# Layer 3 of a graph network kernel: odd key blocks' exponentials added to the even block by an accumulating DMA, sums taken once per pair of blocks, layer 0's residual added by DMA, and a new order of the work

## The chip, the cores and the metric

The kernel runs on one core of a Trainium2 chip. The metric is device time in microseconds (us). The kernel before takes 2258.46 us, the median of three runs (2258.31 to 2259.9). A core has five engines that run side by side, each through its own queue of instructions in order: PE (TensorE, matrix products; its weight loads are listed as PEld), DVE (VectorE), ACT (ScalarE), POOL (GpSimd) and SP (SyncE). Here SP and POOL issue the DMA transfers, which 16 DMA engines carry out.

## The reference

Sixteen graphs of 1024 nodes with 128 features pass through four layers. Each layer ends with `x = layernorm(x + layer(x, adj))`; the adjacency is 0 or 1, about 3% of it ones.

```python
def layer0(X, A, W, a):                       # one head of 128
    H = X @ W
    e = leaky_relu((H @ a[:U])[:, None] + (H @ a[U:])[None, :], 0.2)
    return relu(softmax(e + where(A > 0, 0, -1e9)) @ H)
# layer 1: the same with 8 heads of 16 and elu at the end
# layer 2: mean over the neighbours of x @ W_r, plus x @ self_w.T + self_b, then layernorm, gamma, beta, relu
def layer3(X, A, W):                          # 4 heads of 32
    Wh = einsum('bsf,hfd->bhsd', X, W)
    scores = einsum('bhsd,bhtd->bhst', Wh, Wh) / sqrt(32)
    attn = softmax(where(A > 0, scores, -9e15))
    return einsum('bhst,bhtd->bhsd', attn, Wh)    # heads joined to 128 features
```

## The kernel before

The 1024 nodes are 8 blocks of 128 (`NB = 8`), in two halves of 512. All four layers of a graph work on the same eight mask tiles `m` (one per key block, 8-bit, loaded and converted from `adj` by transfers that POOL issues, L557).

*Layer 0* (`layer0`). DVE makes the weights `z` of each key block (L636), PE multiplies them with `hd` (L648) into two PSUM accumulators `acc1`, ACT divides and applies relu (`share`, L669) into `x1`. DVE then adds the graph's input rows, which SP has loaded into the tile `x0` (L624), by one tensor_tensor per half (L689). The layernorm (`layernorm`: squares L430, `about`, a Newton step, application L468) starts from sums that `share` and the first products give, so it needs no pass of its own for the mean.

*Layer 1* (`layer1`). For each of two groups of 4 heads and each key block DVE makes four `z` of 1024 (L788), and PE multiplies them, four products of 32 columns side by side (L796). Results are copied to `oT1` by ACT (L826), transposed by PE, divided by DVE. *Layer 2* (`layer2`) is products with the masks (L928).

*Layer 3* (`before3`, `layer3`). Queries are taken in two halves of 512. For each key block j: ACT turns the mask into a gap (L1066); PE makes the scores of 4 heads into the two PSUM tiles of the pool `wk` (L1076 for the gap, L1087 for the products); ACT takes their exponentials into two SBUF tiles of the pool `z3`, two heads each (L1123); PE multiplies these tiles (`weighted`, L1102). Keys lie on the partitions, so both the weighted values and the softmax's denominators are products: for each head one with `hh` (32 columns of values) and one with `ones` (32 columns of ones). A tile `acc3` holds two heads, values and denominators in alternate stripes of 32 partitions. After 8 blocks ACT copies both accumulators to `oT3` (L1139), PE transposes them, DVE divides (`share`, L1150 and L1153) and adds the layer's input (L1164).

*Order.* No loop order is written out. Every piece of work is a `step` with an engine, an estimated duration, a due time, the buffers it reads and writes, and a lag after which its results count as there. `Plan.run` simulates the engines with these estimates and emits the instructions in the order in which its simulated engines would start them: of those steps that could start about now, the one with the earliest due time. A pool's places are given out in that simulation too, so which buffer a step uses, and whom it waits for on the chip, comes from it. `SAME` and `URGENT` shift due times (for PE steps of the same kind as the one before, and for ACT and DVE steps that hold PSUM), `LATER1` and `LATER3` those of the products that follow the weights. Consecutive graphs are due `PERIOD` apart, so layer 3 of one graph runs beside layers 0 and 1 of the next. On the chip the emitted order is fixed for each engine; semaphores do the waiting.

The functions with the line numbers of the profile:

Of the kernel before, what the change touches and what calls it, by code (L numbers as in the profile page):

```python
# [24 lines left out]
ALU = mybir.AluOpType  # L25
# [3 lines left out]
P = 128  # L29
HALF = 512  # L30
# [46 lines left out]
class Plan:  # L77
# [8 lines left out]
    SAME = 0.0  # L86
    URGENT = 61.2
    AHEAD = 4322.0
# [136 lines left out]
def tile_binary(  # L225
# [3 lines left out]
    xT_in: bass.AP,  # L229
    adjT: bass.AP,  # L230
# [61 lines left out]
    LATER1 = -3.8  # L292
    LATER3 = 48.7
# [35 lines left out]
    places("z3", 4, [P, 2, HALF])  # L329
    places("oT1", 1, [P, N])  # L330
    places("oT3", 1, [P, N])
    places("x0", 1, [P, NB, P])
# [218 lines left out]
    def before0(b, due):  # L551
        G = graphs[b]
        G["m"] = [Buf("m", f"m_{b}_{j}") for j in range(NB)]
        for j, m in enumerate(G["m"]):
            step(
                "POOL", 0.55, due - 60 + 5 * j,
                lambda m=m, j=j: nc.gpsimd.dma_start(out=m.t, in_=adjT[b, j * P : (j + 1) * P, :]),  # L557
                [], [m], lag=5.0, floor=12.0 + 3 * j if b == 1 else max(due - 60 + 5 * j, 0.0),
            )
        x0 = G["x"] = Buf("x0", f"x0_{b}")  # L560
# [63 lines left out]
        step("SP", 2.0, due, lambda: nc.sync.dma_start(out=x0.t, in_=natural(x[b])), [], [x0], lag=2.5)  # L624

    def layer0(b, due):
# [4 lines left out]
        for half in range(2):  # L631
# [32 lines left out]
            for n in range(2):  # L664
# [23 lines left out]
                "DVE", 0.6, at,  # L688
                lambda ks=ks: nc.vector.tensor_tensor(y.t[:, ks, :], y.t[:, ks, :], G["x"].t[:, ks, :], ALU.add),  # L689
                [G["x"]], [(y, half)],  # L690
# [87 lines left out]
    def layer1(b, due, span):  # L778
# [3 lines left out]
        for g in range(2):  # L782
# [39 lines left out]
            oT, pt, rd = Buf("oT1", "oT1"), Buf("wk", "pb1"), little("rd1", [P, NB, G1, 1])  # L822
# [31 lines left out]
    def last1(b, due):  # L854

        G = graphs[b]
        o, x1, e = G["x2"], G["x1"], Buf("oT1", "e")
# [131 lines left out]
    def before3(b, due):  # L989
# [41 lines left out]
        sq, norms, bound = Buf("oT3", "sq"), little("norms", [P, NB * H3]), little("bound", [P, 1])  # L1031
# [23 lines left out]
    def layer3(b, due, span):  # L1055
# [3 lines left out]
        for half in range(2):  # L1059
            cols = slice(half * HALF, (half + 1) * HALF)  # L1060
            av = [Buf("acc3", f"av3_{g}") for g in range(2)]
# [34 lines left out]
            def weighted(j, g, z, av=av):  # L1096

                for h in range(2):
                    at = D3 * (2 * g + h)
                    for n, lhsT in enumerate((hhs[j // HB].t[:, j % HB, at : at + D3], ones)):  # L1100
                        at = 64 * h + 32 * n
                        nc.tensor.matmul(  # L1102
                            av[g].t[at : at + 32, :],
                            lhsT=lhsT,
                            rhs=z.t[:, h, :],
                            start=j == 0,
                            stop=j == NB - 1,
                        )

            for j in range(NB):  # L1110
# [4 lines left out]
                step("ACT", 0.68, at - 8, lambda j=j, gap=gap, f=missing: f(j, gap), [m[j]], [gap])  # L1115
# [4 lines left out]
                for g in (0, 1):  # L1120
                    step(
                        "ACT", 1.0, at,
                        lambda g=g, sc=sc, zs=zs: nc.scalar.activation(  # L1123
                            zs[g].t.rearrange("p h n -> p (h n)"), sc[g].t, AF.Exp, bias=low.t, scale=S3
                        ),
                        [sc[g], low], [zs[g]],
                    )
                for g in (0, 1):
                    step(
                        "PE", 0.87, at + LATER3, lambda j=j, g=g, z=zs[g], f=weighted: f(j, g, z),  # L1130
                        [zs[g], hhs[j // HB]], [av[g]], mode="32 columns",
                    )
            at = due + span * (half + 1) / 2
            oT, pt, rd = Buf("oT3", "oT3"), Buf("wk", "pb3"), little("rd3", [P, 2 * HB, 2, 1])
            o = Buf("rest", "o3")
            for g in range(2):
                step(
                    "ACT", 0.48, at,
                    lambda g=g, oT=oT, av=av: nc.scalar.copy(oT.t[:, g * HALF : (g + 1) * HALF], av[g].t),  # L1139
                    [av[g]], [(oT, g)],  # L1140
                )
# [6 lines left out]
            def share(pt=pt, rd=rd, o=o):  # L1148
                pn = blocks(pt.t).rearrange("p m (c w) -> p m c w", c=2)
                nc.vector.reciprocal(rd.t, pn[:, :, :, D3 : D3 + 1])  # L1150
                for g in range(2):
                    of_g = slice(g * HB, (g + 1) * HB)
                    nc.vector.tensor_tensor(  # L1153
                        o.t.rearrange("p k (h d) -> p k h d", h=H3)[:, :, 2 * g : 2 * g + 2, :],
                        pn[:, of_g, :, :D3],
                        rd.t[:, of_g].to_broadcast([P, HB, 2, D3]),
                        ALU.mult,
                    )

            step("DVE", 1.07, at, share, [pt], [rd, o])  # L1160
# [22 lines left out]
    PERIOD = 129.0  # L1183
    weights(-198)
    for b in range(B):
        at = b * PERIOD
        at0 = 25 if b == 1 else at
        before0(b, at0 - 50)
        layer0(b, at0)
        before1(b, at + 25)  # L1190
        layer1(b, at + 99, 111)
        last1(b, at + 165)
        layer2(b, at + 165)
        before3(b, at + 223)
        layer3(b, at + 321, 108)
# [579 lines left out]
def tile_adj_resnorm(ctx: ExitStack, tc: tile.TileContext, x, adjT, *weights_and_out, xT):  # L1775
# [3 lines left out]
    tile_binary(tc, x, xT, adjT, *weights_and_out, wrong)  # L1779
# [44 lines left out]
```

## Time and profile before

| | |
|---|---|
| median of three runs | 2258.46 us |
| profiled execution | span 2254.1 us |
| busy, PE / DVE / ACT / POOL | 2074.9 / 1902.1 / 1743.5 / 130.9 us |
| PE products of layer 3 after the exponentials (L1102), with `hh` / with `ones` | 2048 / 2048 rows |
| residual of layer 0 on DVE (L689) | 32 instructions, 683 ns each |
| mask loads (L557) | 128, 540 ns to issue |
| DMA, mean over the span | 53 GB/s |

The profile is one execution. Its span (first to last recorded instruction) is 4.4 us below the median of the runs, which are timed from outside. An engine's busy time is the time in which at least one of its instructions ran. A PE product of 32-bit data appears as two rows. Groups of instructions are listed by line, engine and operation, as output<-inputs, with their count, their busy time, the mean duration of one, then the idle time of the engine just before them and who ended it. In the slices, the span is cut into 40 parts and each digit is a busy share in tenths. The chain is followed back from the last instruction to what released each one.

### The profile page before, as it was taken

The numbers are of one execution on the slowest core, as the hardware profiler recorded it, in microseconds if no ns is written. First come the engines' busy times: TensorE is split into PE (matmuls) and PEld (weight loads), VectorE is DVE, ScalarE is ACT, GpSimd is POOL, SyncE is SP. The second block draws the span as 40 slices with busy tenths as digits, with TensorE's granted clock in tenths as the row PEclk, the third lists the DMA queues.
The fourth block names the chain that finished last, engine by engine and source line by source line (L and its number), as shares of the span: only waits on it lengthen the run. The fifth ranks groups of instructions, "written<-read, shape, count | busy, mean of one in ns | idle before, by whom it ended". The sixth has DMA issues, their size and how long they took to land.

```text
span 2254.1 us, 55458 instructions
## 1 busy us (share of the span) xinstructions
PE 2074.9 (92%) x23472; PEld 971.1 (43%) x23472; DVE 1902.1 (84%) x2854; ACT 1743.5 (77%) x4376; POOL 130.9 (6%) x187
## 2 busy tenths in 40 slices
PE   4857999999999999999999999999999999998876
PEld 4613545353534544363544535353454436242311
DVE  2899999989989989999999998998999999997211
ACT  3413769878787879878787987878787987868786
POOL 1010000100000000000000010000000000000000
PEclk9878999999999999999999999999999999999999
DMA  6122130312323040222314031232304122200000
GB/s 97 59 77 36 37 85 18 92 38 77 48 86 48 20 100 25 86 39 86 48 32 99 18 91 38 77 48 85 50 20 96 29 77 39 77 11 11 2 11 12
DMA packets 80851, 119.86 MB, mean 53 GB/s; under 512 B 7384, under 2 KB 58704, under 8 KB 80592
## 3 DMA queue, kind: packets, MB, share of 16 engines
q1 hardware_dynamic: 62160, 99.43, 13.1%
q0 software_dynamic: 18432, 16.79, 9.0%
q8 instruction: 186, 3.05, 0.6%
q14 instruction: 73, 0.60, 0.1%
HBM read 157.55 MB, written 8.97 MB: 74 GB/s over the span
## 4 chain that ended last, share of the span: by engine, by line
PE 52%; DVE 24%; ACT 20%; issue 3%; DMA 1%; POOL 0%; DVEq 0%; POOLq 0%; ACTq 0%
DVE z L788 18%; PE acc L648 10%; PE acc L1102 9%; PE acc L796 9%; PE wk L928 8%; ACT z L1123 6%; PE wk L1087 6%; PE wk L366 4%; ACT junk L430 4%; ACT x L468 3%; PE wk L375 3%; ACT gap L1066 3%; PE wk L1076 2%; PE wk L1001 1%; ACT hd L620 1%
## 5 line engine op out<-in xcount | busy, mean ns | idle before, releaser
L788 DVE SCALAR_TENSOR_TENSOR z<-R,q,m 128x1024 f32<-128x1024 f32 x1024 | 1248.9, 1279 | 16.1 <-PE acc L796 8.3
L1123 ACT ACTIVATE z<-wk,low 128x1024 f32<-128x1024 f32 x512 | 545.3, 1105 | 58.2 <-PE wk L1087 56.7
L796 PE MATMUL acc<-z,hh 128*32 128x512 f32 x4096 | 512.3, 612 | 46.1 <-DVE z L788 44.6
L1102 PE MATMUL acc<-z,hh 128*32 128x512 f32 x2048 | 516.2, 604 | 33.4 <-ACT z L1123 33.4
L1102 PE MATMUL acc<-z,ones 128*32 128x512 f32 x2048 | 516.1, 604 | 0.0
L430 ACT ACTIVATE junk<-x,off 128x128 f32<-128x128 f32 x640 | 256.2, 400 | 230.8 <-DVE off L424 214.6
L1087 PE MATMUL wk<-whT,turn 32*64 32x512 f32 x4096 | 286.3, 615 | 0.0
L468 ACT ACTIVATE x<-x,shift,rstd 128x128 f32<-128x128 f32 x640 | 259.3, 485 | 7.7 <-DVE shift L462 7.6
L648 PEld LDWEIGHTS acc<-hd,z 128*128 128x128 f32 x2048 | 237.3, 193 | 34.8 <-ACT x L669 12.6
L796 PEld LDWEIGHTS acc<-z,hh 128*32 128x32 f32 x4096 | 110.6, 110 | 326.8 <-issue 194.6
L648 PE MATMUL acc<-hd,z 128*128 128x129 f32 x2048 | 244.7, 278 | 5.9 <-DVE z L636 4.5
L1102 PEld LDWEIGHTS acc<-z,hh 128*32 128x32 f32 x2048 | 97.9, 109 | 279.1 <-issue 190.2
L928 PE MATMUL wk<-y,m 128*128 128x128 bf16 (+1 forms) x3072 | 182.9, 220 | 24.5 <-ACT z L1123 19.9
L1066 ACT ACTIVATE gap<-m,neg_one 128x512 bf16<-128x512 fp8e5 x256 | 183.4, 718 | 20.6 <-DMA m<-in_adj_dram 20.6
L928 PEld LDWEIGHTS <-m 128*128 128x128 fp8e5 x3072 | 181.0, 98 | 37.0 <-issue 27.3
L636 DVE SCALAR_TENSOR_TENSOR z<-R,q,m 128x512 f32<-128x512 f32 x240 | 162.8, 746 | 1.0 <-DMA R<-rows 1.0
L1102 PEld LDWEIGHTS acc<-z,ones 128*32 128x32 f32 x2048 | 97.6, 109 | 83.0 <-issue 83.0
L1076 PEld LDWEIGHTS <-far 32*32 32x32 bf16 x4096 | 35.7, 88 | 210.0 <-issue 198.2
L430 ACT ACTIVATION_READ_ACCUMULATOR junk<-x,off 128x1 f32 x640 | 120.4, 188 | 0.0
L1076 PE MATMUL wk<-gap,far 32*32 32x512 bf16 x4096 | 113.3, 386 | 3.4 <-DVE rest L1153 1.7
L557 POOL DMA_DIRECT2D m<-in_adj_dram x128 | 68.3, 540 | 796.2 <-ACT gap L1066 765.8
L1087 PEld LDWEIGHTS wk<-whT,turn 32*64 32x64 f32 x4096 | 59.8, 130 | 58.6 <-issue 58.6
(119 smaller groups left out, 1859.7 us busy)
## 6 DMA issues: line engine op xcount, KB each, us to landing
R<-rows SPq DMA_DIRECT2D x139, 512.0 KB
m<-in_adj_dram POOLq DMA_DIRECT2D x128, 128.0 KB, 5.6
xT<-in_xT_dram SPq DMA_DIRECT2D x32, 256.0 KB
x<-in_x_dram SPq DMA_DIRECT2D x16, 512.0 KB
out_dram<-x SPq DMA_DIRECT2D x15, 512.0 KB
rows<-rT SPq DMA_DIRECT2D x16, 32.0 KB
out_dram<-x SPq DMA_DIRECT2D x2, 256.0 KB
z<-in_L_gnn_a_dram SPq DMA_DIRECT2D x2, 128.0 KB
```

Source lines behind the costliest of these rows:

```text
L430: nc.scalar.activation(junk.t, y.t[:, k, :], AF.Square, bias=off.t[:, k : k + 1], accum_out=squared.t[:, k : k + 1])
L468: nc.scalar.activation(y.t[:, k, :], y.t[:, k, :], AF.Identity, bias=shift.t[:, k : k + 1], scale=rstd.t[:, k : k + 1])
L636: nc.vector.scalar_tensor_tensor(z.t[:, (j % 2) * HALF : (j % 2 + 1) * HALF], in0=R0.t[:, cols], scalar=q.t[:, j : j + 1], in1=m[j].t[:, c ...
L648: nc.tensor.matmul(av[k // 2].t.rearrange("p (k c) -> p k c", k=2)[:, k % 2, : P + 1], lhsT=z.t[:, at : at + P], rhs=hd.t[:, j, : P + 1], ...
L788: nc.vector.scalar_tensor_tensor(z.t, in0=G["R"][h].t, scalar=q.t[:, j, h : h + 1], in1=m[j].t, op0=ALU.max, op1=ALU.mult)
L796: nc.tensor.matmul(av[half].t[32 * c : 32 * c + 32, :], lhsT=hh.t[:, j, at : at + 32], rhs=zs[c].t[:, half * HALF : (half + 1) * HALF], st ...
L928: nc.tensor.matmul(ps.t[:, k * SLOT : k * SLOT + part.stop - part.start], lhsT=m[j].t[:, rows_i], rhs=y2.t[:, j, part], start=j == 0 and n ...
L1066: nc.scalar.activation(gap.t, m[j].t[:, cols], AF.Square, bias=neg_one, accum_out=squares[:, at : at + 1], saturate=False)
L1076: nc.tensor.matmul(sc[h // 2].t[c * 32 : (c + 1) * 32, (h % 2) * HALF : (h % 2 + 1) * HALF], lhsT=far[rows_r, rows_r], rhs=gap.t[rows_r, : ...
L1087: nc.tensor.matmul(sc[h // 2].t[r * 64 : (r + 1) * 64, (h % 2) * HALF : (h % 2 + 1) * HALF], lhsT=turns[j // HB].t[rows_h, j % HB * P + r ...
L1102: nc.tensor.matmul(av[g].t[at : at + 32, :], lhsT=lhsT, rhs=z.t[:, h, :], start=j == 0, stop=j == NB - 1,)
L1123: lambda g=g, sc=sc, zs=zs: nc.scalar.activation(zs[g].t.rearrange("p h n -> p (h n)"), sc[g].t, AF.Exp, bias=low.t, scale=S3),
```

## The change

In layer 3, the two `z3` tiles of an odd key block are added into those of the even block before it, by an accumulating transfer (`accum_op=ALU.add`) that POOL issues, one per tile. The products with `hh` stay one per block and head; the products with `ones` (now in `totals`) are made once per pair of blocks, from the summed tile. One accumulator now holds the values of all four heads, the other the denominators of all four. So the sum must wait for the even block's own products, and the totals for the sum. The pool `z3` grows from 4 to 6 tiles. The division reads the new layout with one product instead of two. The planner is told that a sum's result is there 5 us after its issue (`SUMMED`).

In layer 0, the residual is added by an accumulating transfer from DRAM straight into the result tile; a copy of `x` in another order, `x_rows`, comes as an input for it. The tile `x0` and its load by SP go, and so do DVE's additions. `oT1` and `oT3` become one tile, `wide`. Due times and the planner's constants have new values, so the order differs on all engines.

```diff
-    SAME = 0.0
-    URGENT = 61.2
+    SAME = 0.48
+    URGENT = 86.07
...
-    LATER1 = -3.8
-    LATER3 = 48.7
+    LATER1 = -0.18
+    LATER3 = 44.44
+    SUMMED = 5.0
...
-    places("z3", 4, [P, 2, HALF])
-    places("oT1", 1, [P, N])
-    places("oT3", 1, [P, N])
-    places("x0", 1, [P, NB, P])
+    places("z3", 6, [P, 2, HALF])
+    places("wide", 1, [P, N])
...
-        step("SP", 2.0, due, lambda: nc.sync.dma_start(out=x0.t, in_=natural(x[b])), [], [x0], lag=2.5)
...
             step(
-                "DVE", 0.6, at,
-                lambda ks=ks: nc.vector.tensor_tensor(y.t[:, ks, :], y.t[:, ks, :], G["x"].t[:, ks, :], ALU.add),
-                [G["x"]], [(y, half)],
+                "POOL", 0.55, at,
+                lambda ks=ks: nc.gpsimd.dma_start(out=y.t[:, ks, :], in_=x_rows[b, :, ks, :], accum_op=ALU.add),
+                [], [(y, half)], lag=SUMMED,
             )
...
-            av = [Buf("acc3", f"av3_{g}") for g in range(2)]
+            av, weights_sum = Buf("acc3", "av3"), Buf("acc3", "sum3")
...
-            def weighted(j, g, z, av=av):
-
-                for h in range(2):
-                    at = D3 * (2 * g + h)
-                    for n, lhsT in enumerate((hhs[j // HB].t[:, j % HB, at : at + D3], ones)):
-                        at = 64 * h + 32 * n
-                        nc.tensor.matmul(
-                            av[g].t[at : at + 32, :],
-                            lhsT=lhsT,
-                            rhs=z.t[:, h, :],
-                            start=j == 0,
-                            stop=j == NB - 1,
-                        )
+            def weighted(j, zs, av=av):
+
+                for h in range(H3):
+                    nc.tensor.matmul(
+                        av.t[32 * h : 32 * h + 32, :],
+                        lhsT=hhs[j // HB].t[:, j % HB, h * D3 : (h + 1) * D3],
+                        rhs=zs[h // 2].t[:, h % 2, :],
+                        start=j == 0,
+                        stop=j == NB - 1,
+                    )
+
+            def totals(j, zs, into=weights_sum):
+
+                for h in range(H3):
+                    nc.tensor.matmul(
+                        into.t[32 * h : 32 * h + 32, :],
+                        lhsT=ones,
+                        rhs=zs[h // 2].t[:, h % 2, :],
+                        start=j == 1,
+                        stop=j == NB - 1,
+                    )
+
+            def added(z, into):
+                nc.gpsimd.dma_start(out=into.t, in_=z.t, accum_op=ALU.add)
...
+                step(
+                    "PE", 0.87, at + LATER3, lambda j=j, zs=zs, f=weighted: f(j, zs),
+                    [*zs, hhs[j // HB]], [av], mode="32 columns",
+                )
+                if j % 2 == 0:
+                    first = zs
+                    continue
                 for g in (0, 1):
                     step(
-                        "PE", 0.87, at + LATER3, lambda j=j, g=g, z=zs[g], f=weighted: f(j, g, z),
-                        [zs[g], hhs[j // HB]], [av[g]], mode="32 columns",
+                        "POOL", 0.55, at + LATER3, lambda z=zs[g], into=first[g], f=added: f(z, into),
+                        [zs[g]], [first[g]], lag=SUMMED,
                     )
+                step(
+                    "PE", 0.87, at + LATER3, lambda j=j, zs=first, f=totals: f(j, zs),
+                    first, [weights_sum], mode="32 columns",
+                )
...
-    PERIOD = 129.0
-    weights(-198)
+    PERIOD = 129
+    weights(-212.32)
     for b in range(B):
         at = b * PERIOD
-        at0 = 25 if b == 1 else at
-        before0(b, at0 - 50)
+        at0 = 34.36 if b == 1 else at
+        before0(b, at0 - 45.69)
         layer0(b, at0)
-        before1(b, at + 25)
-        layer1(b, at + 99, 111)
-        last1(b, at + 165)
-        layer2(b, at + 165)
-        before3(b, at + 223)
-        layer3(b, at + 321, 108)
+        before1(b, at + 25.25)
+        layer1(b, at + 105.52, 106.17)
+        last1(b, at + 189.26)
+        layer2(b, at + 174.65)
+        before3(b, at + 228.67)
+        layer3(b, at + 313.69, 103.74)
...
+    x_rows = given("x_rows", x.reshape(len(x), -1, 128, x.shape[2]).transpose(0, 2, 1, 3))
```

In the changed file these stand at: `weighted` L1097, `totals` L1108, `added` L1117, the exponentials L1132, the residual L687.

## The prediction

> **What bounds the kernel now.** I read the engine totals first, then the slices, then the busy times of one whole cycle in the middle, then the groups, the transfers and the end of the chain. The totals of the page:
>
> ```profile
> span 2254.1 us, 55458 instructions
> ...
> PE 2074.9 (92%) x23472; PEld 971.1 (43%) x23472; DVE 1902.1 (84%) x2854; ACT 1743.5 (77%) x4376; POOL 130.9 (6%) x187
> ...
> PE   4857999999999999999999999999999999998876
> ...
> DMA  6122130312323040222314031232304122200000
> ```
>
> TensorE is full from slice 6 to slice 37; only the filling (first 200 us) and the draining (last 150 us) leave it idle. One reduction on GpSimd (L398 on `bound`) comes once per graph and marks the cycle: it stands at 248.9 us for the first graph, 1928.0 for the 14th, 2056.3 for the 15th, so a graph takes 128.8 us in the middle. The busy times of just such a cycle (PE, PEld, DVE, ACT, POOL, then clock, DMA share, GB/s):
>
> ```profile
> 957.47:1086.25 128.78, 126.26 (x1466) 59.43 (x1462) 118.45 (x178) 108.14 (x274) 8.35 (x11) 1.00 0.25 59
> ```
>
> PE idles 2.5 us of 128.8, DVE 10.3, ACT 20.6. PE sets the pace, DVE stands 8% behind it, the 16 DMA engines are idle three quarters of the time. The groups that the change touches:
>
> ```profile
> L1123 ACT ACTIVATE z<-wk,low 128x1024 f32<-128x1024 f32 x512 | 545.3, 1105 | 58.2 <-PE wk L1087 56.7
> L1102 PE MATMUL acc<-z,hh 128*32 128x512 f32 x2048 | 516.2, 604 | 33.4 <-ACT z L1123 33.4
> L1102 PE MATMUL acc<-z,ones 128*32 128x512 f32 x2048 | 516.1, 604 | 0.0
> ...
> L689 DVE TENSOR_TENSOR x<-x,x 128x512 f32<-128x512 f32 x32 | 21.9, 683 | 1.1 <-ACT x L669 1.1
> ```
>
> The two L1102 rows overlap: four products run side by side, each on its 32 columns. Their joint busy time is 518.6 us. The means of 604 ns must not be multiplied by the counts. What a set of four (8 rows in the trace) costs is in the chain: single sets 0.86 or, after another kind of product, 1.00; two 1.85; three 2.58. So 0.86 each, and 0.14 for a change of kind.
>
> **The change part by part.**
>
> *Products removed.* Before, each key block has 8 products per query half: 4 heads by `hh`, 4 by `ones`, two sets. After, `hh` keeps its set, and `ones` has one per pair of blocks. Per half 4 sets go; 16 graphs x 2 halves x 4 = 128 sets x 0.86 = 110.1 us of PE time, 6.9 us per cycle. A set of four still fills all four column groups, so this is real PE time. The number of changes of kind in PE's order falls by 19 of 928: 19 x 0.14 = 2.7 us, 0.2 per cycle, left out. PE's floor per cycle: 126.3 - 6.9 = 119.4.
>
> *DVE.* The residual add of layer 0 goes (32 x 0.683 = 21.9 us). The division becomes one reciprocal (0.256, same 16 numbers) and one product of 512 (0.690, as L1164) instead of two of 256 (0.420 each): 1.096 to 0.946, 32 x 0.150 = 4.8. Together 26.7 us, 1.7 per cycle: floor 116.8. ACT stays at 108.1.
>
> *Transfers added.* 16 accumulating transfers of 512 KB per graph (8 pairs x 2), all on GpSimd's queue, and two of 256 KB for the residual; the 512 KB load on SP goes. The nearest row is the load of `m`, which also goes out on GpSimd's queue, reads 512 KB and converts on the way:
>
> ```profile
> q1 hardware_dynamic: 62160, 99.43, 13.1%
> q0 software_dynamic: 18432, 16.79, 9.0%
> ...
> L557 POOL DMA_DIRECT2D m<-in_adj_dram x128 | 68.3, 540 | 796.2 <-ACT gap L1066 765.8
> ...
> m<-in_adj_dram POOLq DMA_DIRECT2D x128, 128.0 KB, 5.6
> ```
>
> The columns of the queues are packets, MB and the share of 16 engines' span; L557 has its issue time, the last row KB written and the landing. Issue 0.54 us, landing 5.6 (3.6 to 6.8, median 5.3, in a stretch of 500 us). q0's 9.0% of 2254 us over 128 loads is 1.58 us of all 16 engines for each 512 KB read; q1 gives 1.56. An add may cost the same (512 KB in, 512 KB out), or twice that, since it also reads its destination. 256 of them are 399 to 797 us of engine time: the DMA share goes from 0.23 to between 0.41 and 0.58. Bandwidth is there; latency is the question. POOL gets 288 x 0.54 = 156 us of issues, 13% busy in all.
>
> Two rules bear on the landing. The Trainium skill, "DMA: Bandwidth & Descriptors", section on the anatomy of a SWDGE transfer, fits 2.0 us plus bytes/436e3, which is 3.2 us for 512 KB; the row says 5.6. Against the change speaks "Collectives: The Full Stack", section on the bandwidth ceiling: an adding transfer has two source reads and runs at half a copy's rate. No run here shows that. It would add 1.6 us to the row: 7.2. I take 5.6: both ends are in SBUF, where the row's source is HBM, and the row's loads, too, go out back to back. The range keeps 3.2 and, with the first of a pair still in the way of the second (3.1 more), 10.3.
>
> *The new wait.* Totals can start when the odd block's exponentials are done and added. Counted from the end of the odd block's scores: two exponentials (2.2 us), issue 0.54, landing 5.6: 8.4 us. In the changed program's own order I counted the PE work that stands between the odd block's scores and the totals, at the durations above. Two kinds of graphs alternate. For the first the eight distances are 7.1, 4.4, 10.2, 31.6, 17.1, 21.4, 18.2, 13.1 us; for the second 5.3, 8.5, 14.7, 20.0, 15.6, 27.6, 18.8, 8.0. At 8.4 the first lacks 1.3 + 4.0, the second 3.1 + 0.4: 4.4 us per graph on average. PE takes its queue in order, so behind a waiting total stand the next block's scores, and behind these ACT. But the short distances consist of score batches, and each of those (1.43 us of PE) waits for the wk buffers that the exponentials before it free (2.1 us): real time is longer than counted work. I let half of the lack stand: 2.2 us per cycle. (By 3.2 instead of 5.6, the need is 6.0, the lack 1.15, half of it 0.6.)
>
> *What is behind these steps on GpSimd.* Adds, mask loads, reductions and residuals share one queue in a fixed order. A mask load waits for ACT's last reading of its buffer, up to 39.0 us at a time here, and an add behind it waits too. Both wait for the same ACT queue, so the order costs nothing while ACT keeps its order; its price if it doesn't is one landing, 6 us, per miss. The residual's landing (0.54 + 5.6, instead of 0.68 on DVE) is covered in ACT's order: after the last `share`, ACT has 8 squares, a Newton start, 4 more squares and 8 applications, over 12 us, before it reads that half. The odd blocks' exponentials always use the same two of the six z3 buffers; ACT writes them again one pair later, some 15 us in the middle, so that wait stays hidden up to there. `wide` now serves both layer 1 and layer 3, one buffer where there were two: its holds are a few us in a cycle of 125, priced at nothing; uncovered, a copy behind it is 0.6 us late.
>
> *Middle.* 119.4 + 2.5 (idle as before) + 2.2 = 124.1: 4.7 less than 128.8, 14 times: 65.8 us.
>
> *Ends.* Filling: DVE is the chain there, and graph 0's residual lands 6.1 us after issue instead of 0.68, part of it under `hd` copies of 1.0: +4. Draining: the chain is
>
> ```profile
> 2230.63 1.15 PE wk L1087 x16
> 2231.81 1.12 ACT z L1123
> 2232.97 1.06 PE acc L1102 x8
> 2234.40 1.16 PE wk L1087 x16
> 2235.58 1.12 ACT z L1123
> 2236.75 2.12 PE acc L1102 x16
> 2238.89 0.59 ACT oT L1139
> ```
>
> one block per 3.77 us. Without the second set this may fall to scores 1.4 + two exponentials 2.1 = 3.5, some -4 us over the last 16 blocks; but a pair then lasts 7.0 us, and an add needs 0.54 + 5.6 between the odd exponential and the next one in the same buffer (6.0): it just fits, and I count neither. The very last pair is bare: issue, landing and totals (7.1) instead of 2.1: +5; with the last pair of the half before it, where less is behind, +9 for both.
>
> **Sum.** 2254.1 - 65.8 + 4 + 9 = 2201.3 us of span; the median shown lies 4.4 above the span: 2205.7, so 2206.
>
> **Rivals.** (a) *Everything is kept*: landings near the 3.2 to 4 us end, or all of the lack absorbed. 119.4 + 2.5 = 121.9 per cycle, 14 x 6.9 = 96.6: 2254.1 - 96.6 + 13 + 4.4 = 2175. For: the before's order leaves PE only 2.5 idle. Against: DVE would be at 96%.
> (b) *DVE becomes the bound*: if its 10.3 us of idle are waits that a shorter PE doesn't shorten, the cycle is 116.8 + 10.3 = 127.1, 14 x 1.7 = 24 saved: 2248. For: the z group (L788), DVE's bulk, waits 8.3 us for PE in the whole span; what else idles is short waits in chains through PE and ACT, 1 to 2.5 us each (2.5 for the transposes, 2.2 for ACT, 1.7 for layer 2's products in that cycle). Against: some of these chains start at PE's queue.
> (c) *Slower: the adds land late.* Need 12 us (landing 9.2): the first kind of graph lacks 4.9 + 7.6 + 1.8, the second 6.7 + 3.5 + 4.0, 14.2; half is 7.1, the cycle 129.0, and the sum 2254.1 + 3 + 13 + 4.4 = 2274. It decides from a landing of about 8.4 us on: need 11.2, lack 12, half of it 6.0, which with the ends' 13 us (0.9 per cycle) eats the 6.9. The place is PE's queue at the totals; then the z3 waits of ACT come too. For: two reads per add, two adds at once, bursts of seven 512 KB loads of R. Against: the DMA engines are three quarters idle.
> (d) *Nothing moves*: gain and waits cancel, within 0.2%, about what a measurement of this kernel can tell from no change.
>
> **How the numbers follow.** Forecast 0.42, (a) 0.19, (b) 0.12, (c) 0.23, (d) 0.04. Faster 0.42 + 0.19 + 0.12 = 0.73; same 0.04; slower 0.23. The likeliest case alone spans 2188 to 2232 (none to all of the lack, 14 x 2.2 each way, and the ends). The range runs from 2162, past (a)'s value with the draining's -4 and the changes of kind, to 2274, the value of (c); outside are about a tenth on either side.
>
> **What would show it.** L1108 at half of today's `ones` rows (1024), joint PE time of both lines near 408. The cycle between two L398 on `bound` near 124. z to z transfers landing near 5.6; waits of PE at L1108 on that DMA, two or three per graph, 2 us each. PE near 96% in the middle, DVE 94%. Wrong if landings exceed 8 us, if L1132 waits for the DMA in the middle, or if DVE stays at 10 us idle with a cycle of 127.

## The result: 9.5% slower, and the profile after

The changed kernel takes 2474.55 us (median of 4 runs, 2467.5 to 2480.1) beside 2259.18 us for the kernel before on the same chip: a ratio of 1.0949, with a 95% interval from 1.0925 to 1.0974. The forecast was 2206, and the time lies far outside the range given. From the page of the profile after, the engine totals, the slices and the queues:

```profile
span 2465.5 us, 54179 instructions
...
PE 2120.9 (86%) x22448; PEld 976.9 (40%) x22448; DVE 1891.1 (77%) x2790; ACT 1748.2 (71%) x4376; POOL 360.3 (15%) x475
...
PE   4858897998979899898989989898988989797876
...
PEclk9969999999989999998989999899999999998998
DMA  6130553647456463745556375564637455533445
...
q0 software_dynamic: 59904, 159.41, 39.8%
q1 hardware_dynamic: 45520, 91.04, 11.3%
```

PE has 1024 rows fewer (512 products), and is busy 46 us *longer* (2074.9 before). Its row of nines has become 8 and 9 in turn; its clock (PEclk, in tenths) has eights in the middle, where before it had only nines. No engine is full any more. The groups and transfers of the same page that answer to those shown of before:

```profile
L786 DVE SCALAR_TENSOR_TENSOR z<-R,q,m 128x1024 f32<-128x1024 f32 x1024 | 1250.0, 1279 | 39.0 <-DMA R<-rows 26.9
L1132 ACT ACTIVATE z<-wk,low 128x1024 f32<-128x1024 f32 x512 | 544.6, 1107 | 169.8 <-PE wk L1085 72.6
...
L1117 POOL DMA_DIRECT2D z<-z x256 | 222.3, 941 | 1193.6 <-ACT z L1132 569.5
L1097 PE MATMUL acc<-z,hh 128*32 128x512 f32 x2048 | 309.2, 629 | 0.0
L1108 PE MATMUL acc<-z,ones 128*32 128x512 f32 x1024 | 220.3, 659 | 97.2 <-DMA z<-z 97.1
...
L634 DVE SCALAR_TENSOR_TENSOR z<-R,q,m 128x512 f32<-128x512 f32 x240 | 164.2, 745 | 44.5 <-DMA m<-in_adj_dram 41.1
...
z<-z POOLq DMA_DIRECT2D x256, 512.0 KB, 6.2
R<-rows SPq DMA_DIRECT2D x139, 512.0 KB, 6.4
m<-in_adj_dram POOLq DMA_DIRECT2D x128, 128.0 KB, 7.8
```

The rows of L1108 are halved as the edit says, but L1097 and L1108 together take 529.5 us, not the 408 that were expected. An add lands 6.2 us after its issue (4.5 to 12.9). The masks, which landed after 5.6 us before, now take 7.8.

L398 on `bound` marks the cycle again: first at 251.8 us, last at 2371.7, against 248.9 and 2168.6 before. So filling is 2.9 us longer, draining 8.3 (93.8 from the last mark to the end of the span, 85.5 before), and the 15 cycles between are 200.2 us longer: 13.3 each. All of the surprise lies in the cycles. Two graphs in the middle (PE, PEld, DVE, ACT, POOL, then clock, DMA share, GB/s):

```profile
1104.48:1391.02 286.54, 260.29 (x2800) 119.46 (x2796) 235.45 (x347) 216.80 (x547) 44.63 (x58) 0.95 0.56 112
```

A cycle takes 143.3 us; PE is busy 130.1 of it (119.4 expected) and idle 13.1 (4.7 expected). DMA is busy 0.56 of the time, near the upper end of the 0.41 to 0.58 that the prediction worked out. Who waits for transfers, over the whole span (us, times, longest):

```profile
PEld acc L1108 <- DMA z<-z: 181.9, 87, 5.2
PE acc L1108 <- DMA z<-z: 97.1, 66, 4.3
ACT z L1132 <- DMA z<-z: 65.2, 40, 3.8
...
DVE z L634 <- DMA m<-in_adj_dram: 41.1, 6, 7.9
DVE z L786 <- DMA R<-rows: 26.9, 23, 5.1
ACT gap L1064 <- DMA m<-in_adj_dram: 20.9, 5, 14.5
```

Before, the largest such waits were 20.6 us (the same gap, in the filling), 9.7 and 9.6; DVE waited 6.3 us for R at the same line and never for m. Three kinds of waiting are new or several times longer: PE's for the sums, ACT's for odd tiles whose add still reads them, DVE's for loads that it needs for layers 0 and 1. What one wait of PE does, in PE's timeline (start, duration, then in brackets the idle time before and who ended it); the two adds of this pair were issued from 1106.80 to 1108.55:

```profile
1112.73 1.05 PE L1108 MATMUL acc<-z,ones 128*32 128x512 f32 x4 [1.20 <-DMA z<-z]
1116.07 1.07 PE L1108 MATMUL acc<-z,ones 128*32 128x512 f32 x2 [2.29 <-DMA z<-z]
...
1116.92 1.07 PE L1108 MATMUL acc<-z,ones 128*32 128x512 f32 x2
1116.95 4.45 PE L794 MATMUL acc<-z,hh 128*32 128x512 f32 x14
```

and the same stretch in windows, with the granted clock third from the end:

```profile
1114.00:1116.00 2.00, 0.00 (x0) 0.00 (x0) 2.00 (x3) 0.20 (x1) 0.00 (x0) 0.78 0.10 18
1116.00:1118.00 2.00, 1.93 (x12) 0.62 (x16) 1.27 (x2) 0.00 (x0) 0.00 (x0) 0.50 0.00 0
1118.00:1120.00 2.00, 2.00 (x12) 0.37 (x4) 0.00 (x0) 1.96 (x5) 0.00 (x0) 0.50 0.00 0
1120.00:1122.00 2.00, 2.00 (x8) 0.67 (x5) 0.00 (x0) 0.93 (x3) 0.00 (x0) 0.52 0.00 0
```

Three losses in one stall. Heads 0 and 1 wait for the first transfer, heads 2 and 3 for the second, so that they start 9.3 us after the first was issued: 3.5 us idle in all. The set of four is split in two, and its first half of 4 rows takes 1.05 us, at full clock (1.00 in the windows of 0.5 us around it), as long as a whole set of 8 rows in this view (1.06). And then the clock falls to half: windows of 0.5 us place the fall at about 1115.1 and the return at about 1121.9, 6.8 us later. Meanwhile 14 rows of layer 1's products (L794) take 4.45 us, where 16 rows took 1.92 just before the stall. The Trainium skill, "TensorE: Matmul & The Clock Gate", Part 1 on the HAM clock gate, puts the return to half rate after at least one idle window of about 3.4 us. Here the longest unbroken idle time was 2.3 us, and the clock fell within it, about 3.6 us after the last full set had ended (1111.5); whether the half set in between counts as idling, no run here shows. In the 1500 us from 300 to 1800 the mean clock was 0.96, against 1.00 before. If it has only the two steps seen in this stall, 1.00 and 0.50, that is an estimated 8% of the time at half.

### The profile page after: what moved, and what is told of

The parts are those of the page before. It is cut to its first block, busy times and chain, and to the rows that moved or that the text cites. A ratio compares the mean times of both kernels' runs of the same rounds, so it can differ in the third digit from the quotient of the medians.

```text
span 2465.5 us, 54179 instructions
## 1 busy us (share of the span) xinstructions
PE 2120.9 (86%) x22448; PEld 976.9 (40%) x22448; DVE 1891.1 (77%) x2790; ACT 1748.2 (71%) x4376; POOL 360.3 (15%) x475
## 3 DMA queue, kind: packets, MB, share of 16 engines
q0 software_dynamic: 59904, 159.41, 39.8%
## 5 line engine op out<-in xcount | busy, mean ns | idle before, releaser
L1132 ACT ACTIVATE z<-wk,low 128x1024 f32<-128x1024 f32 x512 | 544.6, 1107 | 169.8 <-PE wk L1085 72.6
L794 PE MATMUL acc<-z,hh 128*32 128x512 f32 x4096 | 562.9, 632 | 62.3 <-DVE z L786 60.9
L430 ACT ACTIVATE junk<-x,off 128x128 f32<-128x128 f32 x640 | 257.4, 402 | 259.1 <-DVE off L424 244.1
L1117 POOL DMA_DIRECT2D z<-z x256 | 222.3, 941 | 1193.6 <-ACT z L1132 569.5
L1097 PE MATMUL acc<-z,hh 128*32 128x512 f32 x2048 | 309.2, 629 | 0.0
L1108 PE MATMUL acc<-z,ones 128*32 128x512 f32 x1024 | 220.3, 659 | 97.2 <-DMA z<-z 97.1
L1085 PE MATMUL wk<-whT,turn 32*64 32x512 f32 x4096 | 295.6, 634 | 0.0
L794 PEld LDWEIGHTS acc<-z,hh 128*32 128x32 f32 x4096 | 116.3, 112 | 384.4 <-issue 229.3
L646 PE MATMUL acc<-hd,z 128*128 128x129 f32 x2048 | 251.7, 280 | 16.0 <-DVE z L634 14.4
L1074 PE MATMUL wk<-gap,far 32*32 32x512 bf16 x4096 | 144.5, 391 | 68.1 <-ACT z L1132 53.0
L1074 PEld LDWEIGHTS <-far 32*32 32x32 bf16 x4096 | 45.6, 88 | 283.8 <-issue 276.7
L1108 PEld LDWEIGHTS acc<-z,ones 128*32 128x32 f32 x1024 | 35.5, 113 | 243.4 <-DMA z<-z 181.9
L1097 PEld LDWEIGHTS acc<-z,hh 128*32 128x32 f32 x2048 | 58.2, 112 | 140.6 <-issue 128.4
L557 POOL DMA_DIRECT2D m<-in_adj_dram x128 | 87.9, 794 | 143.6 <-ACT gap L1064 139.3
```

What stands on the lines that cost most here:

```text
L430: nc.scalar.activation(junk.t, y.t[:, k, :], AF.Square, bias=off.t[:, k : k + 1], accum_out=squared.t[:, k : k + 1])
L646: nc.tensor.matmul(av[k // 2].t.rearrange("p (k c) -> p k c", k=2)[:, k % 2, : P + 1], lhsT=z.t[:, at : at + P], rhs=hd.t[:, j, : P + 1], ...
L794: nc.tensor.matmul(av[half].t[32 * c : 32 * c + 32, :], lhsT=hh.t[:, j, at : at + 32], rhs=zs[c].t[:, half * HALF : (half + 1) * HALF], st ...
L1074: nc.tensor.matmul(sc[h // 2].t[c * 32 : (c + 1) * 32, (h % 2) * HALF : (h % 2 + 1) * HALF], lhsT=far[rows_r, rows_r], rhs=gap.t[rows_r, : ...
L1085: nc.tensor.matmul(sc[h // 2].t[r * 64 : (r + 1) * 64, (h % 2) * HALF : (h % 2 + 1) * HALF], lhsT=turns[j // HB].t[rows_h, j % HB * P + r ...
L1097: nc.tensor.matmul(av.t[32 * h : 32 * h + 32, :], lhsT=hhs[j // HB].t[:, j % HB, h * D3 : (h + 1) * D3], rhs=zs[h // 2].t[:, h % 2, :], st ...
```

## The experiments

Three explanations had to be told apart: *order* (the new due times are slower by themselves, or the freed PE time has no use), *traffic* (the adds hold up other transfers), *waits* (PE and ACT wait for the sums). All ratios are to the kernel before on the same chip, with 95% intervals. In the table, PE idle is the span less PE's busy time; both are from the profiled execution.

| kernel | us | ratio | PE busy | PE idle |
|---|---|---|---|---|
| before | 2259 | 1 | 2074.9 | 179.2 |
| residual by DMA alone, old order | 2264.8 | 1.0009 (1.0002–1.0016) | 2073.6 | 185.7 |
| new due times alone | 2315.5 | 1.0237 (1.0220–1.0254) | 2098.7 | 215.3 |
| changed, no pairs | 2341.3 | 1.0352 (1.0335–1.0369) | 2110.1 | 230.8 |
| changed, adds left out | 2281.3 | 1.0095 (1.0078–1.0111) | 2014.6 | 262.4 |
| changed, adds cut to 1/8 | 2295.7 | 1.0146 (1.0129–1.0163) | 2037.4 | 259.1 |
| changed, copies for adds | 2314.6 | 1.0243 (1.0226–1.0261) | 2046.2 | 269.5 |
| changed, adds that nobody waits for | 2383.2 | 1.0553 (1.0535–1.0570) | 2051.4 | 329.2 |
| changed, totals not waiting | 2394.2 | 1.0588 (1.0570–1.0606) | 2060.3 | 332.5 |
| changed, longer lag planned | 2420.3 | 1.0697 (1.0679–1.0714) | 2082.1 | 335.9 |
| changed | 2474.6 | 1.0949 (1.0925–1.0974) | 2120.9 | 344.6 |
| changed, old due times | 2540.9 | 1.1233 (1.1214–1.1252) | 2155.8 | 385.6 |
| other due times, adds | 2350.7 | 1.0397 (1.0380–1.0414) | 2068.4 | 284.0 |
| other due times, no adds | 2321.7 | 1.0264 (1.0246–1.0283) | 2048.6 | 270.4 |

### Adds left out

```diff
             def added(z, into):
-                nc.gpsimd.dma_start(out=into.t, in_=z.t, accum_op=ALU.add)
+                return
```

> The changed kernel in the same order, with the 256 adding transfers of layer 3 left out; the totals then cover the even blocks alone. If PE's wait for the landings is the cause (with or without the half clock after it), the 200 us and more go: 2170 to 2230 us, PE clock 1.00 in the middle. If the new order or the shared tile `wide` is the cause, it stays above 2330 us. If the transfers' traffic is the cause it is fast too: this run does not tell wait from traffic, the next one does.

Measured 2281.3 us, between the two outcomes expected. The emitted order is that of the changed kernel; what is left out is 256 transfers, so that the totals cover the even blocks alone. So the adds cost 193 us, and *without* them the kernel with half of its `ones` products is still 1% slower than before. Its groups, and behind them two groups of before (L796 is now L794, L1076 is now L1074):

```profile
L794 PE MATMUL acc<-z,hh 128*32 128x512 f32 x4096 | 517.6, 614 | 88.7 <-DVE z L786 88.5
...
L1097 PE MATMUL acc<-z,hh 128*32 128x512 f32 x2048 | 276.7, 605 | 0.0
L1074 PE MATMUL wk<-gap,far 32*32 32x512 bf16 x4096 | 143.2, 388 | 69.7 <-ACT z L1132 56.9 <-DVE rest L894 9.3 <-ACT hh L1024 0.8
L1108 PE MATMUL acc<-z,ones 128*32 128x512 f32 x1024 | 138.3, 610 | 0.0
...
L796 PE MATMUL acc<-z,hh 128*32 128x512 f32 x4096 | 512.3, 612 | 46.1 <-DVE z L788 44.6
L1076 PE MATMUL wk<-gap,far 32*32 32x512 bf16 x4096 | 113.3, 386 | 3.4 <-DVE rest L1153 1.7
```

L1097 and L1108 sum to 415.0: the products are as cheap as forecast. But PE's idle time is 83 us more than before. At L794 it waits 88.5 us for DVE's weights of layer 1 (44.6 before), and at L1074, the first products of a block's scores, 69.7 us (3.4 before), and these same products are busy 143.2 us instead of 113.3. The timeline shows this second place, a score batch (the scores of one key block) cut in two:

```profile
1331.27 1.11 PE L1085 MATMUL wk<-whT,turn 32*64 32x512 f32 x16
1333.84 0.41 PE L1074 MATMUL wk<-gap,far 32*32 32x512 bf16 x8 [1.46 <-ACT z L1132]
1334.84 0.41 PE L1074 MATMUL wk<-gap,far 32*32 32x512 bf16 x8 [0.60 <-ACT z L1132]
```

`wk` has two tiles, and both go to one block's scores. Until ACT has taken their exponentials (2.1 us, here behind other ACT work), PE can't write the next scores. With 8 products per block and half of the queries (4 with `hh`, 4 with `ones`), PE had something to do meanwhile; at the even blocks it now has 4 fewer and arrives early. But most of this waiting has only moved: in the kernel before, PE waited for the same exponentials at the weighted products (L1102, 33.4 us). With the waits of all its lines added up, PE waits for layer 3's exponentials 83.3 us here and 67.0 before, 16 more; its waits for DVE at layer 1's products are 44 longer. So about half of the new idle time is for DVE's weights, though DVE has less work than before (1885.5 us busy, 1902.1 before).

### New due times alone, and the changed kernel without pairs

```diff
+    SAME = 0.48
+    URGENT = 86.07
...
+    LATER3 = 44.44
...
+        layer3(b, at + 313.69, 103.74)
```

> The kernel before with the new due times and constants alone (no pair sums, residual on DVE, oT1 and oT3 apart, four z3 tiles). If the new order is the cause of the 80 us of the run without pairs: 2300 to 2345 us. If `wide` or the six z3 tiles are: below 2275 us.

The kernel before with the changed kernel's constants: 2315.5 us, as expected of a new order that is a cause. By the ratio, this order costs 53 us by itself where the work is unchanged. Taking layer 3's products and division as before but all else of the change (residual by DMA, `wide`, six `z3` tiles, the new due times):

```diff
-                step(
-                    "PE", 0.87, at + LATER3, lambda j=j, zs=first, f=totals: f(j, zs),
-                    first, [weights_sum], mode="32 columns",
-                )
...
+                        "PE", 0.87, at + LATER3, lambda j=j, g=g, z=zs[g], f=weighted: f(j, g, z),
+                        [zs[g], hhs[j // HB]], [av[g]], mode="32 columns",
```

> The changed kernel with layer 3's products as before (ones once per block, no adds); the new due times and constants, the residual by DMA, `wide` and six z3 tiles stay. If the pair sums are the cause: 2240 to 2310 us (within 2.5% of before). If the new order is a cause of its own: above 2350 us.

2341.3 us, between the two outcomes expected. Here PE waits 4.5 us at L1074, busy 115.7, and 45.5 us for the exponentials at the weighted products: that the wait stands at L1074 is the pairs', not the due times'. For DVE at L794 it waits 60.5 us. Putting the pairs in without adds takes PE's busy time from 2110.1 to 2014.6 (95.5 less) and adds 31.6 us of idling: the time falls by 60 us of the 110 counted. The orders of the two differ, since the planner simulates other work; the 60 include that.

### Residual alone, and the old due times

The kernel before, with layer 0's residual as the only edit:

```diff
-                "DVE", 0.6, at,
-                lambda ks=ks: nc.vector.tensor_tensor(y.t[:, ks, :], y.t[:, ks, :], G["x"].t[:, ks, :], ALU.add),
+                "POOL", 0.55, at,
+                lambda ks=ks: nc.gpsimd.dma_start(out=y.t[:, ks, :], in_=x_rows[b, :, ks, :], accum_op=ALU.add),
```

> The kernel before with layer 0's residual alone added by DMA (x_rows, no x0, no DVE addition; due times and constants of before). If the residual's landing is covered as the prediction said: 2250 to 2270 us. If it is a cause of the 80 us of the run without pairs: above 2290 us.

2264.8 us, 1.0009. That the residual's transfer is covered holds. The whole change with the due times of before:

```diff
-    URGENT = 86.07
+    URGENT = 61.2
...
-        layer3(b, at + 313.69, 103.74)
+        layer3(b, at + 321, 108)
```

> The changed kernel's code (pair sums, residual by DMA, `wide`) with all due times and constants of before. If the wait for the landings is the cause, it is slow as well: 2400 to 2550 us. If the new due times are the cause: below 2330 us.

2540.9 us, the slowest of all: the new due times are worth 66 us to the changed kernel, though they cost the old one 53. Here PE waits 115.8 us at L1108 for sums. What an order is worth depends on the work that it orders, so "the order" isn't a separate term of a sum. The changed kernel without adds was not run under the old due times.

### What of an add costs: waits or traffic

First the totals were made from the odd tiles, so that PE waits for no sum (the totals then cover only odd blocks; the adds run as before):

```diff
-                    "PE", 0.87, at + LATER3, lambda j=j, zs=first, f=totals: f(j, zs),
+                    "PE", 0.87, at + LATER3, lambda j=j, zs=zs, f=totals: f(j, zs),
```

> The adding transfers stay, same queue, same bytes, same order, but the products with ones read the odd block's tiles, which the transfers only read; so PE does not wait for a landing, while ACT still does before it writes the tiles again. The totals then cover the odd blocks alone. If the wait in PE's queue is the cause: within 1.5% of the run without adds, 2170 to 2250 us. If the traffic (slower loads of R and m, GpSimd's queue) or ACT's wait for the odd tiles is the cause: above 2350 us.

2394.2 us: taking PE's wait at the totals away gains 80 us. The two profiled spans differ by 73, of which 61 are busy time of PE and 12 idle time. So what PE loses by that wait shows less as idle time than as longer busy time; the split sets and the half clock of the stall above are of this kind. Then ACT's wait was taken too: the even tile is added to itself, so no odd tile is held by an add (totals again of odd blocks only):

```diff
-                nc.gpsimd.dma_start(out=into.t, in_=z.t, accum_op=ALU.add)
+                nc.gpsimd.dma_start(out=into.t, in_=into.t, accum_op=ALU.add)
```

> As the run whose totals read the odd blocks, but each adding transfer takes the even tile as source and destination: same bytes and issues, no engine waits for a landing at PE, and ACT no longer waits for it before it writes the odd tiles. If slower loads of m and R are what the traffic costs: it stays above 2365 us. If ACT's wait for the odd tiles is: 2290 to 2330 us, near the run without adds.

2383.2 us: 11 less, and the trace shows no wait of PE or ACT for an add. So 102 us of the 193 remain when nobody waits for the sums. Two kinds of waiting stand behind them. First in this kernel, then (behind the dots) without adds:

```profile
ACT z L1132 <- PE acc L1108: 72.7, 57, 3.2
PE acc L794 <- DVE z L786: 117.1, 67, 7.2
DVE z L786 <- DMA R<-rows: 63.4, 23, 4.9
DVE z L634 <- DMA m<-in_adj_dram: 41.0, 6, 7.8
...
PE acc L794 <- DVE z L786: 88.5, 64, 5.7
DVE z L786 <- DMA R<-rows: 9.8, 10, 1.9
DVE z L634 <- DMA m<-in_adj_dram: 8.5, 6, 1.8
```

One kind is DVE's waiting for other transfers, and PE's for DVE behind it: R lands after 8.7 us here instead of 5.8, m after 7.3 instead of 5.1. The other comes from the experiment itself: the totals now read the odd tiles, and ACT waits 72.7 us until they have done so (0.3 us in the changed kernel, 51.9 in the run before this one). So the 102 us are not the price of the traffic alone, and how they divide is open; for the same reason 80 and 11 us may be too little for what the two waits cost.

DVE's wait for m in the changed kernel is one load in every second graph, which POOL issues right behind a pair of adds:

```profile
1058.59 1.75 POOL L1117 DMA_DIRECT2D z<-z  x2 [20.09 <-ACT about L448]
1059.70 1.21 POOL L557 DMA_DIRECT2D m<-in_adj_dram  x1
...
1068.09 0.75 DVE L634 SCALAR_TENSOR_TENSOR z<-R,q,m 128x512 f32<-128x512 f32 x1 [6.49 <-DMA m<-in_adj_dram]
```

DVE starts 8.4 us after the load's issue. In the run without adds, the load that DVE waits for there is issued at 1253.90, and DVE starts at 1257.36, 3.5 us later.

To see whether it is the number of transfers or what they move, the adds were cut to 64 of 512 columns per head (the totals then miss most of the odd blocks), and replaced by plain copies of full size (the totals then cover odd blocks only):

```diff
-                nc.gpsimd.dma_start(out=into.t, in_=z.t, accum_op=ALU.add)
+                nc.gpsimd.dma_start(out=into.t[:, :, :64], in_=z.t[:, :, :64], accum_op=ALU.add)
...
+                nc.gpsimd.dma_start(out=into.t, in_=z.t)
```

> The changed kernel with every adding transfer cut to an eighth of its bytes (64 of the 512 columns of each head; the totals then miss most of the odd blocks): same number of issues, same waits, same order. If the bytes make the loss (long service, slower loads of m and R): within 2% of the run without adds, 2280 to 2325 us, landings near 3 to 4 us. If the fixed part of a transfer or GpSimd's queue makes it: above 2390 us.

> The changed kernel with the adding transfers turned into plain copies of the same 512 KB (the totals then cover the odd blocks alone); issues, waits and order stay. If the second read of an adding transfer is what makes it long, the service falls from about 2.8 to about 1.6 us of the 16 engines, the landing to 5 us, and the time to 2330 to 2400 us. If the number of bytes written decides, nothing changes: above 2440 us.

2295.7 us (14 more than without adds) and 2314.6 us (33 more; it was expected at 2330 or above). The same 256 transfers with the same order, and the same instructions behind them, cost 193 as adds, 33 as copies, 14 as short adds. The queue and the landing of the copies, then the queue without adds:

```profile
q0 software_dynamic: 59904, 159.41, 26.1%
...
z<-z POOLq DMA_DIRECT2D x256, 512.0 KB, 3.8
...
q0 software_dynamic: 23040, 25.18, 11.2%
```

q0 counts the same 159.41 MB, but the copies take 26.1% of 2315.7 us where the adds take 39.8% of 2465.5. Less what q0 holds without them (11.2% of 2277.0), that is 349 us over 256, 1.37 us of all 16 engines for a copy, and 726 us, 2.84 us, for an add, if q0's other loads take what they take without them. The prediction quoted from the Trainium skill, "Collectives: The Full Stack", section on the bandwidth ceiling, that an adding transfer runs at half a copy's rate. The page says this of ReduceScatter, whose add needs two source reads; the adds here, within SBUF, agree with it: 2.1 times the service of a copy. The landing, 6.2 against 3.8 us, grows by less.

### Other due times

The planner was first told what the profile shows: 0.88 us for the issue of an add and 7.0 for `SUMMED`.

```diff
-    SUMMED = 5.0
+    SUMMED = 7.0
...
-                        "POOL", 0.55, at + LATER3, lambda z=zs[g], into=first[g], f=added: f(z, into),
+                        "POOL", 0.88, at + LATER3, lambda z=zs[g], into=first[g], f=added: f(z, into),
```

> The changed kernel with the planner told what the profile shows of the adds: 0.88 us of GpSimd for an issue and 7.0 us to the result, instead of 0.55 and 5.0. If totals that stand too early in PE's queue make the last 80 us, PE's wait for the landings falls below 30 us and the time to 2360 to 2420 us. If the wait cannot be ordered away (the buffers of the odd blocks, the traffic): above 2440 us.

2420.3 us, at the slow end of what was expected, 54 less than the changed kernel; but the wait at L1108 (59.1 us, and 107.2 at its weight loads) was not brought under 30, as it should have been. Then all due times were set anew for late sums, with and without the adds:

```diff
-    LATER1 = -0.18
-    LATER3 = 44.44
-    SUMMED = 5.0
+    LATER1 = 14.959
+    LATER3 = 64.772
+    SUMMED = 6.662
...
-                step("ACT", 0.68, at - 8.57, lambda j=j, gap=gap, f=missing: f(j, gap), [m[j]], [gap])
+                step("ACT", 0.68, at + 19.300, lambda j=j, gap=gap, f=missing: f(j, gap), [m[j]], [gap])
...
-    PERIOD = 129
+    PERIOD = 127.831
```

> The changed kernel with other due times throughout: totals and weighted products of layer 3 due 20 us later, the masks' squares (L1064) due 27.9 us later against their block, layer 1 due 16 us earlier, a period of 127.8 instead of 129, 0.88 us for an add's issue and 6.7 us for its way. Nothing is left out. If most of the loss is PE waiting at the totals in a badly fitting order, the waits at L1108 fall from 279 us (181.9 + 97.1) to under 60 and the time to 2200-2260, at or below the kernel before. If the adds' own traffic costs about 100 us through the loads that it holds up, as the adds in place suggest, the waits at L1108 fall as well, but the time stays at 2290-2380. No gain against the changed kernel (over 2450) would say that due times do not matter here.

> The same other due times, with the adds left out (the totals cover even blocks only). If this order suits the shortened work, it shows what the halved products are worth by themselves: 2170-2230, where the order of the changed kernel without adds gave 2281. If an order that leaves long ways for the adds is itself slow, 2260-2300. The difference to the run with the adds is what the adds cost in this order: about 100 us by the traffic theory, under 30 us if only waiting at the totals mattered.

2350.7 us with the adds, 2321.7 without (slower than either outcome expected of it). This decides against a fixed price of the traffic: the adds cost 29 us here, not 100, though q0 is as busy as ever (41.7%) and R lands late, after 7.5 us (4.8 without adds):

```profile
PEld acc L1108 <- DMA z<-z: 32.1, 22, 4.9
ACT z L1132 <- DMA z<-z: 31.1, 19, 4.0
...
PE acc L1108 <- DMA z<-z: 13.9, 11, 4.0
...
DVE z L786 <- DMA R<-rows: 6.5, 4, 5.1
```

A late R holds DVE up by only 6.5 us in this order, and m holds it up nowhere; that their uses stand further from their issues is the likely reason, not a measured one. But the order is slow without the adds as well: without adds it is 40 us slower than the changed kernel's order without adds, at much the same waits of PE at the two places (80.7 us at L794 for DVE, 77.1 in all at L1074); 34 us of the difference are longer busy time of PE, whose mean clock from 300 to 1800 us is 0.97 instead of 0.99. In none of the orders tried did halving the totals beat the kernel before; whether another order would is open.

## Why the prediction was wrong, point by point

*The products.* Right as a busy time: L1097 and L1108 take 415.0 us without adds, 408 expected, 518.6 before. Wrong as a gain. The step that failed is **"119.4 + 2.5 (idle as before)"**. Without any add a cycle of the changed kernel is 129.9 us (two graphs from 1296.2 to 1556.0), not 121.9: PE is busy 122.2 and idle 7.7. So of the 8.0 us by which the cycle is too long, 5.2 are idling and 2.8 PE's busy time. The 2.5 us of idling did not carry over to the new work in its new order. PE waits longer for DVE's weights of layer 1 (88.5 us in the span, 44.6 before) and, by a smaller amount, for layer 3's exponentials (83.3, 67.0 before). The prediction had both in hand: the first as rival (b), the second as score batches that wait for the `wk` tiles, which it used only in the change's favour, as time that would hide the adds. With the order that came along, priced at nothing, this is 8.0 us per cycle, 14 times: 112 of the 268 us missed. How much of it is the order's and how much the work's is open. Nearly all of the rest is the adds: 193 us, where the sum had 31 for the waiting and 9 for the draining.

*Service of an add.* The rule of two reads was quoted and the row of `m` was taken in its place. Measured: 2.84 us of all engines, near the upper end (3.1) rather than the row's 1.58. The landing, 6.2 us, was near the 5.6 taken. What failed is **"Bandwidth is there; latency is the question"**: at a mean DMA share of 0.56 to 0.58, median landings of m rose from 5.1 to 7.3 and 7.8 us and those of R from 5.8 to 6.4 and 8.7, with longer delays at single loads, as at the mask load behind two adds. DVE waits for these loads, and PE for DVE. The prediction asked what the adds wait for, and never what else waits because of the adds; it had the shared queue of GpSimd cost nothing while ACT keeps its order. In this order the adds that nobody waits for still cost about 100 us, of which ACT's new wait in that experiment has an unknown part.

*The new wait.* The kind and place were right (PE at L1108, 66 waits of 1.5 us, four per graph; two or three of 2 us were expected). The size was not: **"two exponentials (2.2 us), issue 0.54, landing 5.6: 8.4 us"** took one landing after one issue. An issue takes 0.87 us (0.54 taken), the second transfer of a pair is issued after the first, and totals need both; in the stall shown, 9.3 us pass from the first issue to the second half's products, where 6.1 were counted. Behind a stall come half-filled sets and half the clock, for which the sum had no term. Taking the wait away gave 80 us; the sum had 2.2 us in 14 cycles, 31 us, for it.

*ACT's wait for odd tiles* was called hidden. It is not (65.2 us, 40 times). Taking it away, with the totals no longer waiting, gave 11 us, but brought ACT more waiting for the totals; what it costs by itself is open.

*Ends.* Draining +8.3 (forecast +9), and for the reason given: without the adds it is 82.9 us, 2.6 less than before. Filling +2.9 (+4), but by luck: the residual was the reason given, and the first mark stands at 247.4 us with the residual alone, 1.5 earlier than before, and at 254.8 with the new due times alone. *The residual* on its own: 1.0009, covered as said. *The span of the likeliest case*, 2188 to 2232, does not follow from its terms: 14 x 2.2 each way from 2206 is 2175 to 2237. *`wide`*, priced at nothing, was not tried alone: all of the change but the pairs stands 26 us above the new due times alone; the residual cost 2 us by itself in the old order, and whether `wide`, the six tiles or the order that follows from them makes these 26 us is open.

*The rivals.* Rival (c) had the sign and the place (the totals in PE's queue, two reads per add), and ended at 2274, for a landing of 9.2 us. It set the point of decision at a landing of 8.4; the kernel lost 215 us at 6.2. Its price was that of PE's waiting alone, without the traffic, the unused time and the clock. Rival (b), that a shorter PE only waits for DVE, is the closest to what the kernel without adds does: 116.8 busy and 10.3 idle for DVE, 127.1 us per cycle, were forecast; 117.4, 12.5 and 129.9 were found.

## What to carry to other kernels

Time taken off the fullest engine is a gain only where the next instruction in its queue is ready earlier: look for what it will wait for (here DVE's weights in layer 1, and two PSUM tiles behind ACT), before multiplying instructions by durations. When work moves to DMA, price it twice, once for those who wait for the new transfer, and once for every load already there that lands later; an add took twice the service of a copy here. Where an order was planned for the old work, compare old and new work each in its own order and in the other's: new due times alone made the old kernel 2.4% slower, and the changed kernel took 2351, 2475 and 2541 us under three sets of them. An experiment that takes one wait away can bring in another; look at all waits of its trace before its difference is called a price.

## What the runs showed of the hardware

- An accumulating transfer of 512 KB within SBUF takes 2.84 us of all 16 engines and lands after 6.2 us; a plain copy of the same tiles 1.37 and 3.8. Its issue on POOL takes about 0.87 us (busy time over count), a copy's 0.535; cut to rows of 256 bytes, an eighth of the bytes, an add lands after 3.3 us but takes longer to issue, 1.22 us.
- A wait of 2.3 us, with 1.2 us of idling and half a set of products just before it, was enough to bring PE's clock to 0.50, and it stayed there for 6.8 us.
- Two products side by side on half of the columns take 1.05 us, four on all of them 1.06 in the same view: a set that is split by a wait is paid about twice. (L1108 is busy 220.3 us in the changed kernel and 138.3 where no add is waited for; a part of that difference is half clock.)
